# Two-layer graph attention on one core: new step lists, a fold in five steps and an earlier check of the last graph

## The chip, the cores and the metric

The kernel runs on one core of a Trainium2 chip. The core has five engines with queues of their own: TensorE (PE: matmuls, with its weight loads shown apart as PEld), VectorE (DVE), ScalarE (ACT), GpSimd (POOL) and SyncE (SP), which here only issues DMAs. An engine takes its instructions strictly in the order in which the program puts them; engines wait for one another by semaphores. The metric is the device time in microseconds (us) of one launch.

## What is computed

64 graphs of 256 nodes with 512 features pass through two layers. Cut to what matters (LN is a layer norm with gains and offsets):

```
Q, K, V = x @ W_q + b_q, x @ W_k + b_k, x @ W_v + b_v         # 8 heads of 64
scores  = Q K^T / 8 + a_i + c_j + log(adj + 1e-9)
x       = softmax(scores) @ V + x                             # layer 0

h       = LN(x; g1, b1) @ W1                                  # 8 heads of 64
e       = leaky_relu(h.a_src1[i] + h.a_dst1[j], 0.2) + adj
x1      = softmax(e) @ h + x                                  # layer 1, first attention
h2      = LN(x1; g2, b2) @ W2                                 # 1 head of 512
out     = softmax(leaky_relu(h2.a_src2[i] + h2.a_dst2[j], 0.2) + adj) @ h2 + x1
```

All of it is in 32-bit floats.

## The kernel before

**Tiling.** A graph's features lie transposed in `xT` (128 partitions x 4 chunks x 256 nodes). Five products with 512x512 weights (V, Q, K, and V1, V2 of the two norms' attentions) are done by `winograd` (from line 309): seven block products instead of eight, each of 256 columns, on three PSUM banks a, b, c. After product 1 ScalarE copies bank a away (`m1`; line 528 for K, 642 for V1 and V2), and product 6 then adds onto the same bank, so TensorE waits there for the copy. Products 1, 5, 2, 6, 3 make the first step of such a product, product 7 the second and product 4 the third ("K", "K7", "K4").

**Steps.** `graph(b)` (from line 480) is a generator: each `yield` ends a step, and one graph has 42 of them: load, turn (transposes of x and adj), V, V7, V4, Q ..., K4, two times scores (16 matmul records each, then four Exps, line 602, on ScalarE), two times mask (line 616, product with adj on DVE), sums 0, product 0 (line 428), gather 0 (line 437 and 441, then the norm's statistics: lines 257 to 264), tokens 1 (a small matmul, line 267, and eight small DVE operations, then a power on GpSimd, line 291, which give `rstd`), V1 ..., rows 1, eight times weights (Relu line 679, sum with adj line 685 on DVE, Exp line 689), sums 1, product 1, gather 1, tokens 2, V2 ..., rows 2, weights 2 (line 747), and two times product 2 (line 759), whose result is scaled on ScalarE (line 767), added on GpSimd (line 768) and stored by SP (line 771).

**Lists.** `start`, `period` and `finish` (from line 775) say in which order the steps of different graphs are traced. In `period` an entry (age, step) stands for the graph that began that many periods ago; the 42 entries run once per graph. TensorE's instructions stay in exactly this order (`tc.manual_schedule`); those of the other engines are ordered by the compiler's own scheduler, which takes the traced order as their priority. So a place in a list is a place in TensorE's queue, and a rank on the other engines and on SP.

**Fold of the norms.** `fold_norm` (from line 165) multiplies W1 and W2 with the norms' gains once, at the start, in three steps: transpose (row vectors by DMA, four products on GpSimd at line 183, four sums on DVE at line 187), columns (32 matmul records, line 199, and several small DMAs) and totals (eight scalings, line 232, `combine`, line 130, and one transpose).

**Check.** The fast path holds only for inputs in a certain range. `skew`, `rinvs` and `seen` collect values that tell it; `note_odd` folds them into `odd`, and the last lines (907 to 912) make `count` from it, which every engine loads at line 915 to run or skip a slower loop over the graphs. `count` is 0 here.

**Buffers** that matter: adj transposed (`AT`) has four, the Exp tiles (`ET`) four, PSUM a ring of eight banks, Q's and K's tiles are reused by the masks' totals.

Of the kernel before, what the change touches and what calls it, by code (L numbers as in the profile page):

```python
# [9 lines left out]
F32 = mybir.dt.float32  # L10
# [4 lines left out]
P = 128  # L15
# [5 lines left out]
def kernel(  # L21
# [69 lines left out]
    skew = const.tile([P, NT], F32, name="skew")  # L91
    nc.gpsimd.memset(skew, LOW)
# [58 lines left out]
    with ExitStack() as main:  # L151
# [13 lines left out]
        def fold_norm(name, w, g, b, sources, targets, heads):  # L165
# [13 lines left out]
            for kk in range(2):  # L179
                blocks = w[:, kk, :4, :HD].rearrange("p (k n) f -> p k n f", n=2)  # L180
                for i, row in enumerate(vectors):
# [4 lines left out]
                    by_head = product.rearrange("p k n f -> p k (n f)")  # L186
                    nc.vector.tensor_reduce(
# [3 lines left out]
            yield  # L191
# [37 lines left out]
            for kc in range(KC):  # L229
                for n in range(2):  # L230
                    block = w[:, kc % 2, BLOCKS[kc // 2, n], :]
                    nc.vector.scalar_tensor_tensor(
                        block, block, g[:, kc : kc + 1], mean[:, n], ALU.mult, ALU.subtract
                    )
            combine(w)
# [131 lines left out]
        def note_ends(ends):  # L367
            v = ends.rearrange("p t i h -> p (t i h)")
            to = small.tile([P, 4 * H], F32, name="unused", tag="unused", bufs=1)
            note(v, AF.Square, to[:, : v.shape[1]])  # L370

        def note_odd(v, low, high):
# [4 lines left out]
            nc.vector.tensor_tensor(bad, bad, v, ALU.not_equal)  # L377
            nc.vector.tensor_reduce(worst, bad, AX.X, ALU.max)
# [101 lines left out]
        def graph(b):  # L480
# [41 lines left out]
            if b > 0:  # L522
                turn_adj()
            left = left_factors(xT, "xS")
# [218 lines left out]
            note_ends(ends)  # L743
# [8 lines left out]
            for t in range(NT):  # L752
                o = X2[:, t, :]

                for n in (1, 0):
# [9 lines left out]
                    cols = slice(n * HD, (n + 1) * HD)  # L765
                    weighted = work.tile([P, HD + H], F32, name="weighted", tag="kept", bufs=4)[:, :HD]
# [3 lines left out]
                for a in range(4):  # L770
                    nc.sync.dma_start(out=rows[a], in_=o[32 * a : 32 * a + 32, :])
# [4 lines left out]
            (3, "V1 4"), (5, "tokens 2"), (2, "scores"), (2, "scores"), (1, "V4"),  # L776
            (3, "rows 1"), (2, "mask"), (5, "V2"), (3, "weights"), (2, "mask"),
            (5, "V2 7"), (2, "sums 0"), (2, "product 0"), (5, "V2 4"), (1, "Q"),
            (5, "rows 2"), (1, "Q7"), (4, "sums 1"), (2, "gather 0"), (3, "weights"),
            (3, "weights"), (3, "weights"), (5, "weights 2"), (4, "product 1"),  # L780
            (0, "turn"), (1, "Q4"), (1, "K"), (1, "K7"), (3, "weights"),
            (5, "product 2"), (1, "K4"), (5, "product 2"), (3, "weights"),
            (2, "tokens 1"), (0, "V"), (2, "V1"), (3, "weights"), (4, "gather 1"),
            (2, "V1 7"), (0, "V7"), (-1, "load"), (3, "weights"),
# [4 lines left out]
            (0, "Q7"), (0, "Q4"), (1, "load"), (1, "turn"), (0, "K"), (0, "K7"),  # L789
            (0, "K4"), (1, "V"), (1, "V7"), (0, "scores"), (0, "scores"), (2, "load"),  # L790
            (0, "mask"), (0, "mask"), (1, "V4"), (1, "Q"), ("w1", "transpose"),
            (0, "sums 0"), (0, "product 0"), (1, "Q7"), (1, "Q4"), (1, "K"), (1, "K7"),
            ("w1", "columns"), (3, "load"), (1, "K4"), (1, "scores"), (0, "gather 0"),
            (2, "turn"), (0, "tokens 1"), ("w1", "totals"), (2, "V"), (0, "V1"),
            (2, "V7"), (0, "V1 7"), (2, "V4"), (0, "V1 4"), (1, "scores"),
            ("w2", "transpose"), ("w2", "columns"), (0, "rows 1"), (1, "mask"),
            (1, "mask"), (3, "turn"), (1, "sums 0"), (0, "weights"), (1, "product 0"),
            (2, "Q"), (2, "Q7"), (4, "load"), (0, "weights"), (0, "weights"),
            (0, "weights"), (0, "weights"), (2, "Q4"), (2, "K"), (1, "gather 0"),
            (2, "K7"), (2, "K4"), (2, "scores"), ("w2", "totals"), (1, "tokens 1"),  # L800
            (3, "V"), (0, "weights"), (0, "weights"), (2, "scores"), (3, "V7"),
            (0, "weights"), (2, "mask"), (1, "V1"), (1, "V1 7"), (0, "sums 1"),
            (1, "V1 4"), (4, "turn"), (1, "rows 1"), (3, "V4"), (2, "mask"),
            (2, "sums 0"), (0, "product 1"), (3, "Q"), (1, "weights"), (2, "product 0"),
            (1, "weights"), (1, "weights"), (3, "Q7"), (3, "Q4"), (2, "gather 0"),
            (1, "weights"), (3, "K"), (1, "weights"), (3, "K7"), (3, "K4"),
            (1, "weights"), (2, "tokens 1"), (4, "V"), (2, "V1"), (1, "weights"),
            (5, "load"), (2, "V1 7"), (1, "weights"), (4, "V7"), (0, "gather 1"),
        ]
        FOLDS = [(w, step) for w in ("w1", "w2") for step in ("transpose", "columns", "totals")]  # L810
# [7 lines left out]
            (-4, "V1 4"), (-6, "tokens 2"), (-3, "scores"), (-3, "scores"), (-6, "V2"),  # L818
            (-3, "mask"), (-3, "mask"), (-6, "V2 7"), (-4, "rows 1"), (-2, "V4"),
            (-4, "weights"), (-3, "sums 0"), (-3, "product 0"), (-6, "V2 4"),  # L820
# [304 lines left out]
```

## Time and profile before

| | us |
|---|---|
| median of 3 runs | 3231.83 (3231.08 to 3232.96) |
| the profiled execution's own time | 3238.18 |
| its span, first to last instruction | 3236.2 |
| mean granted TensorE clock | 0.991 |
| one graph in the middle, V to V of the next, mean of graphs 6 to 55 | 48.67 |
| ScalarE's Relus, line 679: x1024, mean 0.500 | 460.9 busy |
| DVE's sums with adj, line 685: x512, mean 0.711 | 363.3 busy |
| last product of the last graph ends | 3225.13 |

The profile is one execution, so its times are compared with its own 3238.2 us. A timeline line has the start in us from the span's start, the length, the engine, the line of the kernel, the operation, output and inputs by name, shape and count; in brackets the idle time before it and who ended it. Lines of the chain of waits have a start, a length and who held the chain. A line of waits has who waited, for whom, us in all, times and the longest.

### The profile page before, as it was taken

What the parts mean: (1) busy time and instruction counts of PE and PEld (TensorE: products, weight loads), DVE (VectorE), ACT (ScalarE), POOL (GpSimd) and SP (SyncE); (2) the same over time, 40 slices, a digit from 0 to 9 for tenths busy, and PEclk for the clock granted to TensorE, in tenths of its full rate; (3) what the DMA queues carried; (4) which work ended last, traced back from release to release, by engine and by line L of the source; (5) the groups of instructions that cost most, each with busy time, mean ns of one, the idle gap of its engine ahead of it and who ended that gap; (6) DMA issues with size and microseconds to landing.
All of it is one profiled execution on the core that took longest, in us unless ns stands there. A gap on an engine that the chain in (4) does not pass through costs nothing. (4 is left out here: it accounts for less than half of the span.)

```text
span 3236.2 us, 77633 instructions
## 1 busy us (share of the span) xinstructions
PE 3138.6 (97%) x28240; PEld 2627.2 (81%) x28240; DVE 2662.2 (82%) x6025; ACT 2187.6 (68%) x5959; POOL 899.3 (28%) x1250
## 2 busy tenths in 40 slices
PE   7899999999999999999999999999999999999985
PEld 5678888888888888888888888888888888888864
DVE  5888888888888888888888888888888888888874
ACT  3567667667677667677677677677677677677663
POOL 2232232232232232232232232222222222222332
PEclk9999999999999999999999999999999999999998
DMA  4333443443444444444443443444444444444332
GB/s 132 105 115 122 134 132 122 133 131 123 130 132 125 127 136 125 130 131 126 133 132 122 125 134 127 125 133 128 126 130 130 128 128 132 128 129 131 121 110 79
DMA packets 354341, 407.66 MB, mean 126 GB/s; under 512 B 117776, under 2 KB 262176, under 8 KB 353952
## 3 DMA queue, kind: packets, MB, share of 16 engines
q1 hardware_dynamic: 352800, 401.56, 40.4%
q8 instruction: 225, 3.69, 0.5%
q14 instruction: 164, 1.34, 0.1%
q10 hardware_dynamic: 1152, 1.06, 0.1%
HBM read 266.57 MB, written 135.87 MB: 124 GB/s over the span
## 5 line engine op out<-in xcount | busy, mean ns | idle before, releaser
L685 DVE TENSOR_TENSOR ET<-ET,AT 128x512 f32<-128x512 f32 x512 | 363.3, 711 | 241.3 <-ACT ET L679 240.8
L689 ACT ACTIVATE ET<-ET,ends 128x256 f32<-128x256 f32 x1024 | 482.6, 503 | 105.9 <-DVE ET L685 105.0
L679 ACT ACTIVATE ET<-R,f 128x256 f32<-128x256 f32 x1024 | 460.9, 500 | 69.0 <-PE ps_num L428 57.1
L428 PE MATMUL ps_num<-ET,V 128*32 128x256 f32 x8192 | 466.7, 379 | 0.0
L428 PEld LDWEIGHTS ps_num<-ET,V 128*32 128x32 f32 x8192 | 263.9, 110 | 155.1 <-issue 1.0
L301 POOL TENSOR_TENSOR S<-yT 128x256 f32<-128x256 f32 x64 | 47.8, 747 | 1204.3 <-ACT zT L412 1006.5
L768 POOL TENSOR_TENSOR X<-X,weighted 128x256 f32<-128x256 f32 x256 | 211.1, 836 | 574.8 <-ACT weighted L767 574.7
L616 DVE TENSOR_TENSOR ET<-ET,AT 128x1024 f32<-128x1024 f32 x256 | 307.3, 1232 | 36.3 <-ACT ET L602 36.3
L602 ACT ACTIVATE ET<-ps_sc,V 128x512 f32<-128x512 f32 x512 | 302.8, 698 | 7.5 <-PE ps_sc L595 7.4
L325 PE MATMUL ps_a<-w,S 128*128 128x264 f32 (+1 forms) x1024 | 269.6, 386 | 9.4 <-ACT m L642 5.2
L325 PE MATMUL ps_b<-w,S 128*128 128x264 f32 (+1 forms) x1024 | 267.4, 384 | 0.0
L759 PE MATMUL ps_av<-V,ET 128*128 128x258 f32 (+1 forms) x1024 | 251.1, 390 | 10.8 <-DVE ET L747 10.8
L262 DVE BATCH_NORM_STATS2 parts<-Z 128x6 f32<-128x128 f32 x1024 | 245.5, 277 | 0.0
L595 PE MATMUL ps_sc<-QT,KT 64*128 64x256 f32 x2048 | 239.4, 383 | 0.0
L325 PEld LDWEIGHTS ps_a<-w,S 128*128 128x128 f32 x1024 | 189.0, 190 | 48.7 <-ACT m L642 8.6
L325 PEld LDWEIGHTS ps_b<-w,S 128*128 128x128 f32 x1024 | 194.6, 190 | 31.4
L759 PEld LDWEIGHTS ps_av<-V,ET 128*128 128x128 f32 x1024 | 190.0, 196 | 35.3 <-DVE ET L747 11.3
L595 PEld LDWEIGHTS ps_sc<-QT,KT 64*128 64x128 f32 x2048 | 192.5, 187 | 25.0 <-issue 1.7
L649 ACT ACTIVATE V<-ps_a,rstd 128x257 f32<-128x257 f32 (+1 forms) x128 | 60.1, 470 | 199.9 <-PE ps_a L325 199.9
L437 DVE TENSOR_TENSOR ps_num<-ps_num,R 128x512 f32<-128x512 f32 x256 | 169.6, 687 | 4.3 <-DMA R<-kept 4.1
L767 ACT ACTIVATE weighted<-ps_av,rinvs 128x256 f32<-128x256 f32 x256 | 114.4, 472 | 76.8 <-DVE rinvs L764 60.4
L332 PE MATMUL ps_a<-S,wk 128*128 128x128 f32 x1024 | 148.1, 288 | 14.1 <-ACT m L528 13.6
(176 smaller groups left out, 7193.0 us busy)
## 6 DMA issues: line engine op xcount, KB each, us to landing
R<-kept SPq DMA_DIRECT2D x128, 512.0 KB
X<-in_x_dram SPq DMA_DIRECT2D x256, 128.0 KB
kept<-xT SPq DMA_DIRECT2D x64, 512.0 KB
yT<-kept SPq DMA_DIRECT2D x64, 512.0 KB
R<-kept SPq DMA_DIRECT2D x512, 64.0 KB
kept<-yT SPq DMA_DIRECT2D x64, 512.0 KB
kept<-Z SPq DMA_DIRECT2D x64, 512.0 KB
X<-kept SPq DMA_DIRECT2D x512, 64.0 KB
```

What stands on the lines that cost most here:

```text
L262: nc.vector.bn_stats(parts[:, block].rearrange("p h c -> p (h c)"), Z[:, block, :])
L325: nc.tensor.matmul(to, A[:, kk, :], B[:, kk, :], start=(first and kk == 0), stop=(kk == 1), skip_group_check=not first,)
L428: nc.tensor.matmul(num[32 * a : 32 * a + 32, m * N : (m + 1) * N], V[:, j, a // 2, a % 2 * P + q * DH + 32 * m :][:, :32], pair[a // 2][:, ...
L437: nc.vector.tensor_tensor(both, both, R[:, q, :].unsqueeze(1).to_broadcast([P, 2, N]), ALU.mult)
L595: nc.tensor.matmul(banks[h % 2][:, o : o + N], KT[lo : lo + DH, (q + h) // 2, j * P : (j + 1) * P], QT[lo : lo + DH, (q + h) // 2, :], sta ...
L602: nc.scalar.activation(ET[:, j, i::2, :], banks[i].rearrange("p (h n) -> p h n", n=N), AF.Exp, bias=c[:, j, :],)
L616: nc.vector.tensor_tensor(ET[:, j, :, :], ET[:, j, :, :], AT[:, j, :].unsqueeze(1).to_broadcast([P, 4, N]), ALU.mult,)
L679: nc.scalar.activation(ET[:, j, h, :], R[q][:, h, :], AF.Relu, bias=f[:, j, at : at + 1])
L685: nc.vector.tensor_tensor(two, two, AT[:, j, :].unsqueeze(1).to_broadcast([P, 2, N]), ALU.add)
L689: nc.scalar.activation(ET[:, j, i, :], ET[:, j, i, :], AF.Exp, bias=targets[:, j, 4 * q + i : 4 * q + i + 1],)
L759: nc.tensor.matmul(av[:, :width], ET[:, j, t * P : (t + 1) * P], V2[:, j, n, :width], start=(j == 0), stop=(j == NT - 1),)
L768: nc.gpsimd.tensor_tensor(o[:, cols], o[:, cols], weighted, ALU.add)
```

## The change

It changes the following.

- **Fold.** The first step is cut in two (one half of the chunks each: transpose, products), and so is the last (scale, totals). For W2 (one head) the four sums over 1024 elements on DVE become eight ScalarE instructions over 512 elements with an accumulator.
- **Lists.** `start`, `period` and `finish` are new. In `period` one scores step stands between V and V1, tokens 1 stands ahead of the second product 2, and load, turn, mask, weights, gather, rows and weights 2 have other places; nearly all ages are lower by one (load's is not, and one scores step's is lower by two).
- **Last graph.** Its product 2 is scaled and added by one DVE instruction straight from PSUM, and half of its stores are issued by ScalarE. `skew` becomes part of `latest`, with two more columns for the last graph: the largest element of AT, and the sum of squares of its `ends`. They are compared with `limits` after weights 2 (`note_latest`), the larger checks come once all other graphs are traced, and `count` is made ahead of the last product 2.

```diff
+    latest = const.tile([P, NT + 2], F32, name="latest")
+    nc.gpsimd.memset(latest, LOW)
+    skew = latest[:, :NT]
+    limits = const.tile([P, NT + 2], F32, name="limits")
+    nc.gpsimd.memset(limits, 0.0)
+    nc.gpsimd.memset(limits[:, NT : NT + 1], 400.0)
+    nc.gpsimd.memset(limits[:, NT + 1 :], 30.0)
...
                     by_head = product.rearrange("p k n f -> p k (n f)")
+                    if heads == 1:
+                        for k in range(2):
+                            nc.scalar.activation(
+                                by_head[:, k], by_head[:, k], AF.Identity,
+                                accum_out=w[:, kk, 2 * k + i, HD:],
+                            )
+                        continue
                     nc.vector.tensor_reduce(
...
-            yield
+                yield
...
                         block, block, g[:, kc : kc + 1], mean[:, n], ALU.mult, ALU.subtract
                     )
+                if kc == 1:
+                    yield
...
+        def note_latest():
+
+            bad = work.tile([P, HD + H], F32, name="bad", tag="kept", bufs=4)[:, : NT + 2]
+            worst = small.tile([P, 1], F32, name="worst", tag="worst")
+            nc.vector.tensor_tensor(bad, latest, limits, ALU.min)
+            nc.vector.tensor_tensor(bad, bad, latest, ALU.not_equal)
+            nc.vector.tensor_reduce(worst, bad, AX.X, ALU.max)
+            nc.vector.tensor_tensor(odd, odd, worst, ALU.max)
...
+            if last:
+                nc.vector.tensor_reduce(
+                    latest[:, NT + 1 :], AT.rearrange("p j n -> p (j n)"), AX.X, ALU.max
+                )
...
-            note_ends(ends)
+            note_ends(ends, latest[:, NT : NT + 1] if last else None)
...
+                    if last:
+                        nc.vector.scalar_tensor_tensor(
+                            o[:, cols], av[:, :HD], rinv[:, t : t + 1], o[:, cols],
+                            ALU.mult, ALU.add,
+                        )
+                        continue
...
-                    nc.sync.dma_start(out=rows[a], in_=o[32 * a : 32 * a + 32, :])
+                    queue = nc.scalar if last and a % 2 else nc.sync
+                    queue.dma_start(out=rows[a], in_=o[32 * a : 32 * a + 32, :])
...
         period = [
-            (3, "V1 4"), (5, "tokens 2"), (2, "scores"), (2, "scores"), (1, "V4"),
-            (3, "rows 1"), (2, "mask"), (5, "V2"), (3, "weights"), (2, "mask"),
-            (5, "V2 7"), (2, "sums 0"), (2, "product 0"), (5, "V2 4"), (1, "Q"),
-            (5, "rows 2"), (1, "Q7"), (4, "sums 1"), (2, "gather 0"), (3, "weights"),
-            (3, "weights"), (3, "weights"), (5, "weights 2"), (4, "product 1"),
-            (0, "turn"), (1, "Q4"), (1, "K"), (1, "K7"), (3, "weights"),
-            (5, "product 2"), (1, "K4"), (5, "product 2"), (3, "weights"),
-            (2, "tokens 1"), (0, "V"), (2, "V1"), (3, "weights"), (4, "gather 1"),
-            (2, "V1 7"), (0, "V7"), (-1, "load"), (3, "weights"),
+            (2, "V1 4"), (4, "tokens 2"), (-1, "load"), (1, "scores"), (1, "mask"),
+            (3, "weights"), (0, "V4"), (1, "mask"), (4, "V2"), (4, "V2 7"),
+            (2, "rows 1"), (2, "weights"), (1, "sums 0"), (1, "product 0"), (4, "V2 4"),
+            (0, "Q"), (4, "rows 2"), (0, "Q7"), (2, "weights"), (2, "weights"),
+            (3, "sums 1"), (1, "gather 0"), (3, "product 1"), (2, "weights"), (0, "Q4"),
+            (-1, "turn"), (4, "weights 2"), (0, "K"), (0, "K7"), (4, "product 2"),
+            (0, "K4"), (1, "tokens 1"), (2, "weights"), (2, "weights"),
+            (4, "product 2"), (-1, "V"), (0, "scores"), (2, "weights"), (1, "V1"),
+            (3, "gather 1"), (1, "V1 7"), (-1, "V7"),
         ]
...
         start = [
             (0, "load"), (0, "turn"), (0, "V"), (0, "V7"), (0, "V4"), (0, "Q"),
-            (0, "Q7"), (0, "Q4"), (1, "load"), (1, "turn"), (0, "K"), (0, "K7"),
-            (0, "K4"), (1, "V"), (1, "V7"), (0, "scores"), (0, "scores"), (2, "load"),
-            (0, "mask"), (0, "mask"), (1, "V4"), (1, "Q"), ("w1", "transpose"),
-            (0, "sums 0"), (0, "product 0"), (1, "Q7"), (1, "Q4"), (1, "K"), (1, "K7"),
-            ("w1", "columns"), (3, "load"), (1, "K4"), (1, "scores"), (0, "gather 0"),
-            (2, "turn"), (0, "tokens 1"), ("w1", "totals"), (2, "V"), (0, "V1"),
-            (2, "V7"), (0, "V1 7"), (2, "V4"), (0, "V1 4"), (1, "scores"),
-            ("w2", "transpose"), ("w2", "columns"), (0, "rows 1"), (1, "mask"),
+            (1, "load"), (0, "Q7"), (1, "turn"), (0, "Q4"), (0, "K"), (0, "K7"),
+            (0, "K4"), (1, "V"), (2, "load"), (1, "V7"), (0, "scores"), (1, "V4"),
+            (0, "scores"), ("w1", "transpose"), (0, "mask"), (0, "mask"), (1, "Q"),
+            (0, "sums 0"), ("w1", "products"), (1, "Q7"), (0, "product 0"), (1, "Q4"),
+            (1, "K"), (1, "K7"), ("w1", "columns"), (0, "gather 0"), (2, "turn"),
+            ("w1", "scale"), (1, "K4"), (1, "scores"), (0, "tokens 1"),
+            ("w1", "totals"), (2, "V"), (0, "V1"), (2, "V7"), (0, "V1 7"), (3, "load"),
+            ("w2", "transpose"), (2, "V4"), (0, "V1 4"), ("w2", "products"),
+            (1, "scores"), (3, "turn"), (1, "mask"), (1, "mask"), (4, "load"),
+            ("w2", "columns"), (1, "sums 0"), (0, "rows 1"), (0, "weights"),
...
         finish = [
...
-            (-1, "mask"), (-1, "sums 0"), (-1, "product 0"), (-4, "V2 4"),
-            (-4, "rows 2"), (-3, "sums 1"), (-1, "gather 0"), (-2, "weights"),
-            (-2, "weights"), (-3, "product 1"), (-2, "weights"), (-4, "weights 2"),
-            (-2, "weights"), (-4, "product 2"), (-4, "product 2"), (-1, "tokens 1"),
-            (-1, "V1"), (-1, "V1 7"), (-2, "weights"), (-3, "gather 1"),
-            (-2, "weights"), (-1, "V1 4"), (-2, "weights"), (-1, "rows 1"),
-            (-3, "tokens 2"), (-2, "weights"), (-3, "V2"), (-3, "V2 7"), (-2, "sums 1"),
-            (-3, "V2 4"), (-1, "weights"), (-1, "weights"), (-1, "weights"),
-            (-1, "weights"), (-3, "rows 2"), (-3, "weights 2"), (-2, "product 1"),
+            (-3, "weights"), (-4, "V2 7"), (-1, "sums 0"), (-1, "product 0"),
+            (-3, "weights"), (-4, "V2 4"), (-4, "rows 2"), (-3, "sums 1"),
+            (-3, "product 1"), (-2, "weights"), (-1, "gather 0"), (-1, "tokens 1"),
+            (-4, "weights 2"), (-3, "gather 1"), (-2, "weights"), (-4, "product 2"),
+            (-2, "weights"), (-2, "weights"), (-2, "weights"), (-4, "product 2"),
+            (-1, "V1"), (-1, "V1 7"), (-1, "V1 4"), (-2, "weights"), (-1, "rows 1"),
+            (-1, "weights"), (-1, "weights"), (-2, "weights"), (-3, "tokens 2"),
+            (-3, "V2"), (-1, "weights"), (-3, "V2 7"), (-2, "weights"), (-3, "V2 4"),
+            (-1, "weights"), (-3, "rows 2"), (-2, "sums 1"), (-2, "product 1"),
...
         ]
...
-                if (g, name) == (B - 1, "rows 2"):
-
-                    note_odd(rinvs[:, : NT * (B - 8)], 1e-25, 1e25)
+                steps_left[g] -= 1
+                others = sum(n for of, n in steps_left.items() if of != B - 1)
+                passed = passed or (g, name) == (B - 1, "V2")
+                if passed and not others and not noted:
+                    noted = True
+                    note_odd(rinvs[:, : NT * (B - 1)], 1e-25, 1e25)
                     note_odd(seen[:, : 4 * B], -1.0, 1e25)
-                    note_odd(seen[:, 4 * B :], -1.0, 3600.0)
+                    note_odd(seen[:, 4 * B : 6 * B - 1], -1.0, 3600.0)
+                if (g, name) == (B - 1, "weights 2"):
+                    note_latest()
+                if steps_left[B - 1] == 1 and not counted:
+                    assert noted
+                    counted = True
+                    pt = ps("tr")
+                    nc.tensor.transpose(pt[:1, :P], odd, ident)
+                    nc.vector.tensor_reduce(odd[:1, :], pt[:1, :P], AX.X, ALU.max)
+                    nc.vector.tensor_scalar(count[:1, :], odd[:1, :], float(B), None, ALU.mult)
         for g in graphs.values():
             assert next(g, None) is None
-        note_odd(skew, LOW, 0.0)
-        note_odd(rinvs[:, NT * (B - 8) :], 1e-25, 1e25)
-        count = const.tile([P, 1], mybir.dt.int32, name="count")
-        pt = ps("tr")
-        nc.tensor.transpose(pt[:1, :P], odd, ident)
-        nc.vector.tensor_reduce(odd[:1, :], pt[:1, :P], AX.X, ALU.max)
-        nc.vector.tensor_scalar(count[:1, :], odd[:1, :], float(B), None, ALU.mult)
```

The rest of `start` and `finish` holds the same steps in a like order.

## The prediction

> **What bounds the kernel now.** I read the page's totals first, then the windows by stage, then what TensorE waits for, and last the order of its work.
>
> ```profile
> PE 3138.6 (97%) x28240; PEld 2627.2 (81%) x28240; DVE 2662.2 (82%) x6025; ACT 2187.6 (68%) x5959; POOL 899.3 (28%) x1250
> ```
>
> TensorE is busy for 97% of the span, so at most about 98 us could be won without touching a matmul. The windows say where those microseconds are (span from:to, length, then busy us of PE, PEld, DVE, ACT, POOL; granted clock; DMA):
>
> ```profile
> 50.00:100.00 50.00, 37.62 (x310) 29.80 (x309) 39.36 (x65) 15.68 (x41) 26.11 (x17) 0.94 0.33 102
> 100.00:150.00 50.00, 43.55 (x377) 34.47 (x379) 42.66 (x78) 31.37 (x79) 9.28 (x11) 0.93 0.27 88
> ...
> 2500.00:2900.00 400.00, 398.17 (x3641) 335.41 (x3631) 338.92 (x771) 283.16 (x776) 111.31 (x156) 1.00 0.42 130
> ...
> 3100.00:3150.00 50.00, 39.86 (x326) 29.48 (x324) 38.09 (x95) 32.56 (x84) 16.14 (x16) 0.90 0.36 116
> 3150.00:3200.00 50.00, 33.83 (x289) 23.94 (x288) 27.50 (x70) 24.98 (x71) 12.28 (x15) 0.90 0.31 96
> ```
>
> The long middle is full; the first 150 us and the last 140 us are not. What TensorE waited for (total us, times, longest):
>
> ```profile
> PE ps_st L267 <- DVE parts L264: 19.6, 4, 8.2
> PE ps_a L332 <- ACT m L528: 13.6, 22, 1.9
> PE ps_av L759 <- DVE ET L747: 10.8, 4, 6.1
> ```
>
> Asked by window, the first and third lie in the start and the finish; the second is the whole loss of the middle.
>
> TensorE's instructions follow the hand-written lists, so counting them in order gives the start of every step of every graph. One graph takes 48.67 us (mean, graphs 6 to 55), 48.32 at best. Adding the median distance from each step's first matmul to the next one's, with K at its shortest (4.466 us), gives 48.08. So 0.59 us a graph is lost, 0.56 of it in step K (57 graphs, mean 5.03). The cause in one period:
>
> ```profile
> 313.36 1.70 ACT L679 ACTIVATE ET<-R,f 128x256 f32<-128x256 f32 x4
> 314.97 0.89 ACT L689 ACTIVATE ET<-ET,ends 128x256 f32<-128x256 f32 x2
> 315.76 0.60 ACT L561 ACTIVATE QT<-ps_a,columns 128x128 f32<-128x128 f32 x2
> 316.26 0.36 ACT L528 COPY m<-ps_a 128x256 f32<-128x256 f32 x1
> ```
>
> K's product 6 reuses K's first bank, which ScalarE must have copied (L528). That copy stands behind Relus and Exps of "weights" and behind Q4's L561; the bank was complete at about 314.9, the copy ended at 316.6.
>
> **The period: what it costs.** The list is the old one with ages one lower, and on TensorE only two steps change place. One "scores" leaves the pair and goes between V and V1; "tokens 1" goes ahead of the second product 2. A pair and a single of the old trace (TensorE in time order):
>
> ```profile
> 45.77 3.73 PE L595 MATMUL ps_sc<-QT,KT 64*128 64x256 f32 x32
> 49.42 1.14 PE L325 MATMUL ps_a<-wv,xT 128*128 128x257 f32 x4
> ...
> 3113.33 2.00 PE L595 MATMUL ps_sc<-QT,KT 64*128 64x256 f32 x16
> 3115.26 1.13 PE L325 MATMUL ps_a<-w,zT 128*128 128x257 f32 x4
> ```
>
> A pair holds TensorE 3.65 us, a single 1.93, so two singles cost 0.20 more. The step before scores also ends later (V to scores 4.497 us once, against V to V1 4.404), +0.09, and the first product after it takes 0.971 instead of 0.867, +0.10. Together +0.40. V no longer follows the 48-wide matmul of tokens 1 and should take 4.34 instead of 4.40: -0.07. **Floor 48.41, +0.33 a graph**, over about 58 periods +19 us. Here the Trainium skill speaks against the change: "TensorEngine Tiling (Array Packing)", Key Properties, says that changing the tiling mode drains the array. Scores use 64 rows, their neighbours 128, and the split adds two changes. The page gives no price; by the one drain that another page prices, about 128 cycles at 2.4 GHz ("TensorE: Matmul & The Clock Gate", Part 2), two would be an estimated 0.11 us a graph, 6 us in all. The rows have 0.40; I take the rows, since they hold the same shapes.
>
> **The period: what it may bring.** K's wait is bounded at -0.59 (gone) and, if ScalarE's order gets worse, +0.4 (K took 1 us too long in the worse old graphs). I take -0.42. In the old list the fifth weights step stands right after K7 and its Relus run just ahead of K's copy; the new list has no weights step between Q4 and tokens 1, and two of the other four come before "gather 0", so their DVE halves no longer wait behind eight bn_stats of 0.28 us. Also four of the scores' eight Exps (0.57 us each) leave the stretch after tokens 2, and half of the mask work can start sooner, where DVE is full. Net -0.09 a graph: **-5 us**, between -15 and +42.
>
> Three margins of the new order I checked against the rows. Tokens 2 to V2's product 6 shrinks from 7.5 to 5.7 us; rstd ended 3.2 us after tokens 2 in all 50 graphs, and a 0.54 us copy follows: it fits. K4 to V stays at 1.9 us (product 2 and tokens 1 change places) and two xT transposes of 0.67 need 1.35. The "weights 2" step now follows "turn", whose transposes take 2.2 us on DVE; its L747 ended 4.1 us ahead of product 2 in the old order, so some 1.5 us are left. The "load" moves from the list's end to its third place, behind the eight X2 issues of tokens 2 on SP: 24.6 us of TensorE's work ahead of turn instead of 26.5, for X and A that are 2 us of issues each.
>
> **The start.** TensorE waits there, between 60 and 150 us: 3.8 for the fold of W1 (L199), 6.3 for parts (L264), 4.1 for the ACT copy u (L642), 3.0 for the totals (L621), and 1.5 in small ones; after such waits the matmuls run slow, so that from 47.6 to 143.9 us it falls 29.6 us behind the sum of its steps. The change: (a) the W1 fold moves ahead of graph 0's masks and W2's loads move up with (2, load). SP issued the vectors only at 57.8 behind 11.0 us of W2's sixteen DMAs; POOL's products (4 x 2.36 us) began at 61.7, having been idle for 20.7. Begun some 5 us sooner, the 3.8 us wait goes. Behind those DMAs SP holds graph 1's rows and A, not late yet. (b) Layer two's sums leave DVE: 4 x 1.20 us (L187) at 97.5 to 105.8, in a stretch where DVE has hardly any idle time from 73.5 to 104. They become eight ScalarE instructions of 128x512; nearest row 0.72 (L520) plus 0.19 to read the accumulator, 7.3 us on an engine with 31.4 of 50 busy: hidden, and if not, up to 2 us. (c) Steps of five spread DVE's scaling (8 x 0.48) and combining (4 x 0.7, up to 2.7 beside POOL), ahead of which gather 0 now stands: the 4.0 us wait for tokens 1 shrinks. Bounds: -20 (waits and half of the slow clock) and +4 (the sums land before a ScalarE copy). I take **-9**: the 3.8, half of u's and parts' 8.1, and 1 of slow clock.
>
> **The finish.** TensorE's order hardly changes: counted in work left to the end, every step of the last graph's matmuls stays within 1 us but V4, K7 and tokens 1. Tokens 1 now stands ahead of the two product 2 that waited 6.1 us for L747 anyway (parts ready 3136.9, L747 3136.8), so V1 no longer waits for rstd: it took 6.3 us instead of 4.45, -1.9. V2 4 of graph 61 loses its cover (sums 1), +0.6, and sums 1 of graph 62 comes after rows 2 of 61; its R had about 5 us to spare before L437 took it up at 3172.9. The large checks move into V2, where DVE had 4.2 us idle: -0.3. The waits of 8.2 and 5.1 for parts are one chain on DVE that nothing shortens. Sum **-2**, between -8 and +6.
>
> **The tail.** Columns: start, length.
>
> ```profile
> 3225.83 0.70 DVE odd L379
> 3226.53 0.04 issue
> 3226.57 0.28 PE ps_tr L910
> 3226.86 0.02 issue
> 3226.88 0.29 DVE odd L911
> 3227.17 0.02 issue
> 3227.19 0.14 DVE count L912
> ```
>
> TensorE's last product ends at 3225.13; every engine then loads the count at 3227.37, and from there TensorE's branches (3.34 and 2.4 us) carry the end to 3236.2. With the count made ahead, that load follows the last product: -2.2. The transpose between the products costs +0.3; odd is ready, since four DVE operations of 0.15 us follow weights 2 and a product 2 of 3.2 us lies between. ScalarE's 0.47, POOL's 0.72 and two of four 0.43 us DMA issues after the last product become one DVE operation of 0.5: beside TensorE's branches, nothing; behind the two DMAs that wait on ScalarE's queue stands only its load of the count. Graph 63's maximum over AT is one reduce of about 0.6 us: nothing. **-2**.
>
> **Sum**: -5 -9 -2 -2 = -18. The profiled execution took 3238.2 (span 3236.2); against it 3220, against the median of 3231.8 **3213**.
>
> **Rivals.** (1) K's wait stays, since ScalarE's order is left to the scheduler: -5 becomes +19, 3237.5. For it: Q4's copies still follow the fourth weights step. (2) Slower: the early scores' Exps (0.57 us each) get in front of V's and V1's copies on ScalarE, and TensorE waits for one of them in every graph, 0.6 us: 3213 + 35 = 3248. It turns the sign from 0.32 us a graph on. For it: those copies leave little margin, and eight PSUM banks must hold V, scores and V1; against: ScalarE was mostly idle in that stretch. (3) Start and finish give nothing, because a fold begun sooner meets a DVE that is full anyway: 3213 + 11 = 3224. (4) All of K's wait goes and the start gives 18: 3213 - 10 - 9 = 3194.
>
> **How the numbers follow.** Forecast 0.43, (1) 0.17, (2) 0.20, (3) 0.08, (4) 0.12. What this kernel's runs tell from no change is 0.2%, 6.5 us. Faster: forecast, (4) and part of (3), 0.58; same: most of (1), part of (3), 0.19; slower: (2) and the rest of (1), 0.23. Range 3195 to 3246; the forecast's own 3200 to 3226.
>
> **What would show it.** Right: K without L528 waits, a period of 48.4 to 48.6, single scores of 1.93, L199 without a wait, the count ahead of the last L759. Wrong: a wait that recurs in every graph at V, V1 or product 2, or a period above 49.

## The result, and the profile after

| us | before | after |
|---|---|---|
| median, lowest to highest, runs side by side | 3232.39 (3231.08 to 3236.77), 6 runs | 3247.33 (3243.28 to 3250.74), 6 runs |
| the profiled execution: time, span | 3238.18, 3236.2 | 3243.28, 3241.5 |
| a second profiled execution: time, span | 3230.90, 3228.9 | 3242.43, 3240.7 |

The changed kernel is slower: ratio 1.0042, 95% interval 1.0032 to 1.0053, some 15 us; a second comparison gave 1.0038, 1.0024 to 1.0052. The forecast was 18 us faster. The traces themselves differ by less than the medians: 8.5 us, when the two executions of each kernel are averaged. These are the changed kernel's totals, and what its TensorE waited for (total us, times, longest):

```profile
PE 3161.7 (98%) x28240; PEld 2614.3 (81%) x28240; DVE 2655.7 (82%) x6022; ACT 2201.4 (68%) x5971; POOL 896.5 (28%) x1249
```

```profile
PE ps_st L281 <- DVE parts L278: 25.6, 5, 9.1
PE ps_a L346 <- ACT m L558: 9.1, 19, 1.1
...
PE ps_a L339 <- DVE V L570: 3.6, 2, 3.1
...
PE ps_fold L211 <- ACT left L207: 2.4, 1, 2.4
```

Line 558 is the old line 528: K's wait is still there, 9.1 us in 19 graphs where it was 13.6 in 22. TensorE is busy 23 us longer with the same 28240 matmuls. That is the first sign that the loss is no wait at all. The windows (from:to, length, busy us of PE, PEld, DVE, ACT, POOL, then granted clock and DMA) show it again:

```profile
50.00:100.00 50.00, 39.92 (x322) 31.16 (x319) 36.87 (x65) 18.30 (x47) 26.90 (x17) 0.93 0.36 104
100.00:150.00 50.00, 42.83 (x377) 33.84 (x376) 39.34 (x74) 34.79 (x93) 7.96 (x11) 0.93 0.30 91
...
2500.00:2900.00 400.00, 398.29 (x3620) 331.03 (x3610) 331.08 (x753) 280.38 (x768) 108.10 (x152) 1.00 0.41 127
```

In the 400 us of the middle TensorE is as full as before, at full clock, and issues 21 matmuls fewer (3620, before 3641). The start is a little denser: 322 and 377 matmuls in its two windows, before 310 and 377. TensorE's steps, counted in list order, give the ledger. Each figure is the mean of the two executions of a kernel; the last column is the forecast's term.

| stretch, us | before | after | difference | forecast |
|---|---|---|---|---|
| start to V4 of graph 5 | 242.3 | 239.4 | -2.9 | -9 |
| V4 of graph 5 to V4 of graph 58 | 2578.4 | 2596.3 | +17.9 | about -5 |
| from there to TensorE's last product | 400.6 | 399.0 | -1.6 | -2 |
| TensorE's last product to the span's end | 11.2 | 6.4 | -4.8 | -2 |

The split of the two scores steps fills the second row. TensorE of the changed kernel, in order of time, around the two scores of one graph:

```profile
471.92 1.03 PE L339 MATMUL ps_b<-wv,S 128*128 128x257 f32 x4
472.88 2.00 PE L625 MATMUL ps_sc<-QT,KT 64*128 64x256 f32 x16
474.80 1.16 PE L339 MATMUL ps_a<-w,yT 128*128 128x264 f32 x4
...
482.00 0.32 PE L281 MATMUL ps_st<-parts,same 128*128 128x48 f32 x2
482.25 2.00 PE L625 MATMUL ps_sc<-QT,KT 64*128 64x256 f32 x16
484.18 1.13 PE L339 MATMUL ps_a<-wv,xT 128*128 128x257 f32 x4
```

From first matmul to the next step's first, both scores take 1.92 to 1.93 us (474.80 - 472.88, 484.18 - 482.25); in a pair they take 1.83 each. No bracket with idle time stands in any of these lines: the loss is inside busy time.

### The profile page after: what moved, and what is told of

It reads as the page before. It is cut to its first block, busy times and chain, and to the rows that moved or that the text cites. A ratio compares the mean times of both kernels' runs of the same rounds, so it can differ in the third digit from the quotient of the medians.

```text
span 3241.5 us, 77524 instructions
## 1 busy us (share of the span) xinstructions
PE 3161.7 (98%) x28240; PEld 2614.3 (81%) x28240; DVE 2655.7 (82%) x6022; ACT 2201.4 (68%) x5971; POOL 896.5 (28%) x1249
## 3 DMA queue, kind: packets, MB, share of 16 engines
q10 hardware_dynamic: 1344, 1.33, 0.1%
## 4 chain that ended last, share of the span: by engine, by line
PE 86%; DMA 4%; ACT 4%; DVE 2%; issue 0%; SPq 0%; POOL 0%; DVEq 0%; ACTq 0%
PE ps_a L339 21%; PE ps_a L346 13%; PE ps_num L454 10%; PE ps_b L339 10%; PE ps_sc L625 7%; PE ps_av L789 7%; PE ps_b L346 6%; PE ps_c L339 5%; PE ps_su L413 4%; DMA R<-kept 4%; PE ps_c L346 3%; ACT ET L709 2%; ACT ET L719 1%; PE ps_st L281 1%; ACT QT L591 0%
## 5 line engine op out<-in xcount | busy, mean ns | idle before, releaser
L719 ACT ACTIVATE ET<-ET,ends 128x256 f32<-128x256 f32 x1024 | 475.9, 503 | 101.4 <-DVE ET L715 101.3
L625 PE MATMUL ps_sc<-QT,KT 64*128 64x256 f32 x2048 | 256.9, 390 | 0.0
L438 ACT ACTIVATE yT<-yT,columns 128x256 f32<-128x256 f32 x256 | 120.9, 499 | 77.4 <-DMA yT<-kept 77.4
L315 POOL TENSOR_TENSOR S<-zT 128x256 f32<-128x256 f32 x63 | 48.7, 773 | 447.5 <-PE ps_a L339 442.4
```

Of the source, the lines that this page charges most:

```text
L625: nc.tensor.matmul(banks[h % 2][:, o : o + N], KT[lo : lo + DH, (q + h) // 2, j * P : (j + 1) * P], QT[lo : lo + DH, (q + h) // 2, :], sta ...
L719: nc.scalar.activation(ET[:, j, i, :], ET[:, j, i, :], AF.Exp, bias=targets[:, j, 4 * q + i : 4 * q + i + 1],)
```

## The experiments

The letters in the expectations: A, the split of the scores costs TensorE its time; C, K waits for Q4's copies; E and F, K waits because R lands late.

**The split alone.** The changed kernel with the pair put back, and the kernel before with nothing but the split:

```diff
+        for g in range(4, 60):                      # e1_pair, on the changed kernel
+            order.remove((g, "scores"))
+            order.insert(order.index((g, "scores")), (g, "scores"))
+        for g in range(5, 60):                      # e2_split, on the kernel before
+            order.remove((g, "scores"))
+            order.insert(order.index((g + 1, "V")) + 1, (g, "scores"))
```

> The changed kernel with the two scores steps of graphs 4 to 59 next to each other again; all else of the change stays. Theory A (each split of the pair costs TensorE 0.40 us in tile-mode changes, and that is what made the change slower): the graph-to-graph time falls from 48.98 to about 48.6 us, 56 graphs x 0.40 = -22 us, so about 3225 us, 7 below the kernel before. Rival B (the new ranks of weights, gather and mask on ScalarE and DVE are what costs; the split is hidden): the time stays at 3243 to 3250 us.

> The kernel before with one change: the first scores step of graphs 5 to 59 stands after the next graph's V, as in the new period. Theory A: +0.40 us a graph for 55 graphs, about 3254 us, single scores of 1.93 us. Rival B: no more than 3 us slower, about 3233 us.

With the pair back the changed kernel took 3233.52 us, 0.9990 of before (0.9979 to 1.0000), and its mean period 48.70 us in place of 48.98. The split alone took 3260.23, ratio 1.0074 (1.0059 to 1.0090): 24 us, against 55 graphs times the 0.40 us of the forecast, 22. Its best period rose from 48.32 to 48.74. So the split is the loss, shown from both sides, and the rest of the change is worth about 3 us (0 to 7). The pair brought back 17 us and not the 22 of the forecast: scores, V and V1 fell by 0.20, 0.10 and 0.12 us a graph, but K's mean was 5.07 us, 0.13 above the first trace of the changed kernel. With the new lists and the pair together, then, K waits as long as before the change.

**The code without the new lists**, that is before's three lists with the new fold steps next to their old neighbours, and **Q4 behind K's products** in the kernel before:

```diff
+        for g in range(4, 62):                      # e4_q4
+            order.remove((g, "Q4"))
+            order.insert(order.index((g, "K")) + 1, (g, "Q4"))
```

> The changed kernel's code (fold in five steps with its new steps next to their old neighbours, layer two's sums on ScalarE, last graph's check and stores) with the three lists of before. If the lists alone cost and the code alone gains: the end after the last product shrinks from 11.1 to about 6.6 us and the sums leave DVE, -4 to -8 us, about 3226 us. If the code costs too (ScalarE's sums in front of copies): 3232 us or more.

> The kernel before with step Q4 of graphs 4 to 61 moved from ahead of K to behind K's first five products; TensorE's work is the same. Theory C (K's product 6 waits because Q4's two ScalarE copies, 0.6 us, stand in front of the copy of K's first bank): K's excess falls from 0.56 to 0.2 us or less a graph, -15 to -25 us, about 3212 us. Rival D (the Exps of the fourth weights step alone hold the copy up): K's excess stays above 0.45 us, 3226 to 3236 us.

The code alone: 3236.20 us, ratio 0.9997 (0.9989 to 1.0006); its tail was 8.1 us in place of 11.2 and its start 1 us later (V2 of graph 5 at 438.5, before 437.5). Q4 moved: 3236.92, 0.9999 (0.9988 to 1.0010), K's mean 5.18 us in place of 5.05. Theory C falls: K waits just as long when Q4's copies no longer stand in front.

**What K waits for.** Two graphs of the kernel before, one after the other. ScalarE, then TensorE, in order of time; the brackets hold the idle time before a line and who ended it:

```profile
1722.05 1.69 ACT L679 ACTIVATE ET<-R,f 128x256 f32<-128x256 f32 x4
1723.64 0.89 ACT L689 ACTIVATE ET<-ET,ends 128x256 f32<-128x256 f32 x2
1724.44 0.60 ACT L561 ACTIVATE QT<-ps_a,columns 128x128 f32<-128x128 f32 x2
1724.94 0.36 ACT L528 COPY m<-ps_a 128x256 f32<-128x256 f32 x1
...
1770.14 0.91 ACT L689 ACTIVATE ET<-ET,ends 128x256 f32<-128x256 f32 x2 [0.65 <-DVE ET L685]
1772.38 1.71 ACT L679 ACTIVATE ET<-R,f 128x256 f32<-128x256 f32 x4 [1.33 <-DMA R<-kept]
1773.99 0.89 ACT L689 ACTIVATE ET<-ET,ends 128x256 f32<-128x256 f32 x2
1774.79 0.60 ACT L561 ACTIVATE QT<-ps_a,columns 128x128 f32<-128x128 f32 x2
1775.29 0.36 ACT L528 COPY m<-ps_a 128x256 f32<-128x256 f32 x1
```

```profile
1725.35 1.16 PE L332 MATMUL ps_a<-S,wk 128*128 128x128 f32 x8
...
1775.70 0.49 PE L332 MATMUL ps_a<-S,wk 128*128 128x128 f32 x2 [1.95 <-ACT m L528]
```

The order on ScalarE is the same in both graphs. In the second, ScalarE has stood 0.65 us for VectorE, and then its Relus of heads 4 to 7 stand 1.33 us before an R that has not landed; K's copy stands behind both, and TensorE pays 1.95 us. R alone is the usual case, and it holds in every graph of 6 to 55: each wait of TensorE above 0.15 us has a wait for R on ScalarE right ahead of it (1.07 after 1.03, 0.78 after 0.74, 0.63 after 0.59), and graphs without the one have less than 0.12 of the other. (In the second executions it holds in 17 of 19 such graphs of before and 17 of 17 of the changed kernel; in the other two ScalarE was late after a wait of 0.6 us for VectorE.) In the changed kernel the order and the wait are the same (here graph 48; graph 21: 1.05 after 1.02):

```profile
2367.66 1.71 ACT L709 ACTIVATE ET<-R,f 128x256 f32<-128x256 f32 x4 [0.88 <-DMA R<-kept]
2370.98 1.16 PE L346 MATMUL ps_a<-S,wk 128*128 128x128 f32 x8 [0.92 <-ACT m L558]
```

R is issued on SP (L476) only when sums 1 has freed its buffer, and that hardly varies: in the first trace of before the issue stands about 4.3 us ahead of K, and the Relus come up for it as a rule 3.8 us after the issue. What varies is the landing. The trace has it in sixteen parts: the last landed 3.4 to 5.8 us after the issue, the fifteenth never later than 4.3. In the graph with 1.95 us, fifteen had landed after 3.8 us and the last after 5.8. Why one part is late in some graphs stays open.

**R sooner, by a fourth buffer** (X2 gives up one for the space, which e8 tries alone; two of the fold's vectors move to another buffer):

```diff
-    [P, n, N], F32, name="R", tag="R" if n == 4 else "R1", bufs=3 if n == 4 else 1
+    [P, n, N], F32, name="R", tag="R" if n == 4 else "R1", bufs=4 if n == 4 else 1
-            X2 = data.tile([P, NT, D], F32, name="X2", tag="X2", bufs=2)
+            X2 = data.tile([P, NT, D], F32, name="X2", tag="X2")
```

> The kernel before with a fourth buffer for the row tiles R, so that the second half of rows 1 need not wait for sums 1; the room comes from X2, which has one buffer instead of two. Theory E (TensorE waits in K because ScalarE, in order, waits for the transfer R<-kept, which is issued only when sums 1 frees the third buffer): the waits on the ACT copy of K's bank vanish, K falls from 5.05 to about 4.7 us a graph, -20 us, about 0.994 of the time before. Rival F (the transfer is late whenever it is issued, by contention): K stays at 5.0 us or more and the time within 3 us.

> The changed kernel with the scores pair restored in graphs 4 to 59 and the fourth R buffer. If the split's tile-mode changes and the late R are the two costs of the middle and they add: e1_pair's time less some 20 us, about 0.993 of the time before; a period of 48.4 us. If E is wrong: as e1_pair, 0.999.

> The changed kernel with the fourth R buffer, the split left in. Theory A and E together: K's wait goes, the single scores stay at 1.93 us, the period is 48.7 to 48.8 us, about 23 us slower than e6_pair_r4 and about equal to the kernel before. If the split hid behind K's wait, it would now be nearer to e6_pair_r4 than 15 us.

> Control for e5_r4: the kernel before with X2 in one buffer and three R buffers as before. All theories: no change, within 3 us of the kernel before; K at 5.0 to 5.15 us.

TensorE's waits in e5_r4, and ScalarE's wait for R, from 400 to 2900 us (total, times, longest):

```profile
PE ps_a L332 <- ACT m L561: 44.9, 50, 2.3
PE ps_a L332 <- ACT u L561: 25.8, 48, 0.5
PE ps_a L332 <- ACT m L528: 1.9, 4, 0.8
```

```profile
ACT ET L679 <- DMA R<-kept: 137.1, 50, 4.2
```

K's wait is gone, 1.9 us where it was 12.4, and yet the kernel is slower by a ratio of 1.037 (1.0352 to 1.0387). The wait for R has moved and grown: the scheduler that orders ScalarE now puts Relus ahead of Q's copies, where R has not landed either, so ScalarE stands before it for 137.1 us in place of 9.3, and Q took 6.33 us in place of 4.46 on average. That is the same mechanism in another place. It does not show what K would gain from an R that is there in time, since R's issue and ScalarE's order changed together. On the changed kernel the buffer gave 1.0325 with the pair and 1.0452 without (1.0310 to 1.0341, 1.0435 to 1.0468), a difference of 41 us for the split where the three-buffer kernels show about 17. Most of the excess is in V1, 4.96 us against 4.45 with the pair, where the split costs 0.12 with three buffers; why stays open. The control without the fourth buffer: 1.0007 (0.9997 to 1.0018).

**The Relus later.** Not the data but the order: the Relus of heads 4 to 7 are queued on ScalarE behind the second copy of K.

```diff
...
+                    behind = k_copies.get(b + 2) if q == 1 else None
+                    with tc.issue_after(behind.ins) if behind else nullcontext():
+                        for j in range(NT):
+                            nc.scalar.activation(
+                                ET[:, j, h, :], R[q][:, h, :], AF.Relu, bias=f[:, j, at : at + 1]
+                            )
...
```

> The kernel before with one constraint on ScalarE's order and nothing else: the Relus of a graph's heads 4 to 7 (the ones that need the second R) are queued behind the first two copies of the K product of the graph two later. Theory F (K's wait is ScalarE standing in its queue before a Relu whose R has not landed): K on TensorE falls from a mean of 5.05 us to 4.8 or less, the waits on the copy m L528 in 400 to 2900 us fall from 12.4 us to under 2, the mean period from 48.7 to 48.35-48.45, the time by 58 x 0.3 = 17 us to about 3220 (ratio 0.9945). Rival G (the delayed Relus are themselves needed: the wait only moves, to K's third copy, to the copies of V or to sums 1 of the next period): period within 0.1 of 48.7 or above, a new row of 10 us or more among TensorE's waits, ratio 1.000 or above.

> The changed kernel with both scores products of a graph put side by side again (graphs 4 to 59) and with the Relus of heads 4 to 7 queued behind the first two copies of K. Theory F: the two add up; the kernel with the pair alone stood at 0.999 of before, K's wait was 0.36 us per graph in it, so about 58 x 0.3 = 17 us less: ratio 0.9935 (3216 us), period 48.35-48.45, scores 1.83 each. Rival G: ratio 0.998 to 1.003, period 48.7, K short but a new wait elsewhere.

TensorE's waits in e9_pin, and one of ScalarE's, from 400 to 2900 us:

```profile
PE ps_a L326 <- ACT m L649: 33.7, 49, 0.7
PE ps_a L326 <- DVE V L658: 26.6, 49, 0.9
PE ps_a L333 <- ACT u L533: 14.8, 49, 0.3
...
PE ps_a L333 <- ACT m L533: 3.4, 8, 1.1
```

```profile
ACT yT L413 <- DMA yT<-kept: 162.7, 49, 4.2
```

Rival G, and far beyond it: 1.0396 (1.0382 to 1.0410). K's first copy costs 3.4 us in place of 12.4, but V1 takes 0.95 us more and V7 0.71 in every graph, and Q and K itself 0.22 each on average. With the pair in the changed kernel it was 1.0339 (1.0323 to 1.0355); there V7 alone lost 1.73 us a graph to VectorE (L688). ScalarE's order changed far beyond the Relus: it now stands 162.7 us before the load of yT, 12.1 before. So these runs show what the constraint costs, and not what K's wait is worth; by which chain the delayed Relus reach V1 and V7 was not traced.

**The same data in two halves**, so that the first Relus need only the first:

```diff
-                nc.sync.dma_start(out=R, in_=kept[q : q + n, :].partition_broadcast(P))
+                step = 2 if q == 4 else n
+                for k in range(0, n, step):
+                    nc.sync.dma_start(
+                        out=R[:, k : k + step], in_=kept[q + k : q + k + step, :].partition_broadcast(P))
```

> The kernel before with the load of the second R (heads 4 to 7, 512 KB) issued as two loads of two heads each and nothing else; ScalarE's order stays as it was but for one Relu a place earlier. Theory F (K waits because ScalarE stands before the first Relu of heads 4 to 7 until R has landed): the first half lands about 1 us sooner than the whole, K on TensorE falls from 5.05-5.17 to 4.8-4.9, the waits on m L528 (its line moves by a few) fall from 12.4 us to 3-6, the time by 58 x 0.2 = 12 us (ratio 0.996). Rival J (a load's landing is set by its fixed part, or by the queue of the DMA engines, not by its bytes): the halves land when the whole did, one more issue on SP costs 0.4 us per graph that nobody waits for: ratio 0.999 to 1.002, K unchanged.

> The changed kernel with the pair of scores side by side and R's second load in two halves. Theory F: the pair's 0.999 and 12 us less: ratio 0.995 (3217 us), scores 1.83, K 4.8 to 4.9. Rival J: 0.999, as with the pair alone.

ScalarE's wait for R in the kernel before, then in e13_halves, and TensorE's in e13_halves, from 400 to 2900 us:

```profile
ACT ET L679 <- DMA R<-kept: 9.3, 18, 1.3
```

```profile
ACT ET L684 <- DMA R<-kept: 30.8, 48, 1.3
```

```profile
PE ps_a L332 <- ACT u L533: 15.5, 51, 0.5
PE ps_a L332 <- ACT m L533: 15.3, 39, 1.1
```

Both expectations missed: 1.0106 (1.0091 to 1.0122), and 1.0082 (1.0068 to 1.0095) on the changed kernel with the pair. The first half did land sooner, 3.3 us after its issue (median), the second 4.2. But the first Relu now stands two Exps earlier, so it comes up for its half about 1.2 us sooner, and ScalarE waits for R in nearly every graph. K's mean rose by 0.48 us, and 0.40 of it is something else: one Relu more stands ahead of K's third copy, so that the last of K's five products takes 1.35 us in place of 0.95. So this run, too, changed ScalarE's order along with the data. What carries the account of K's wait is the match from graph to graph, in both kernels; no experiment took the wait away with ScalarE's order left as it was.

**The start: the fold's vectors on another queue**, in the changed kernel, and all of it together:

```diff
-                nc.sync.dma_start(out=row, in_=a.rearrange("h d -> (h d)").partition_broadcast(P))
+                nc.scalar.dma_start(out=row, in_=a.rearrange("h d -> (h d)").partition_broadcast(P))
```

> The changed kernel with the fold's four vector loads on ScalarE's DMA queue in place of SP's, so that they do not stand behind W2's sixteen pieces. Theory H (the start gave 3 us and not 9 because the vectors still came late): POOL's first product begins at 52 us or earlier in place of 62.3, the waits on w1's columns on TensorE fall from 3.7 us to under 1, the first V2 of graph 5 begins 3 us earlier, the time is about 3 us under the changed kernel's (ratio to before 1.003). Rival I (another wait of the start takes its place: V4 of graph 2 behind VectorE, the parts of the statistics): products earlier, but V2 of graph 5 within 1 us of the changed kernel's, ratio 1.004 to 1.005; a loss if the loads delay ScalarE's first copies or if the products take VectorE's time earlier.

> All three: the changed kernel with the pair of scores, the Relus behind K's copies and the vectors on ScalarE's queue. Theory F with H: ratio 0.9925 (3212 us). F with I: 0.9935, as without the vectors. G: 0.998 or above.

First SP and POOL of the changed kernel, then POOL and VectorE of e11_vec:

```profile
47.16 11.15 SPq L128 DMA_DIRECT2D w<-in_L_gnn_W_dram  x16
58.35 0.58 SPq L182 DMA_DIRECT2D vector<-in_L_gnn_a_src_dram  x1
...
59.51 0.54 SPq L422 DMA_DIRECT2D kept<-inverse  x1
```

```profile
62.30 6.97 POOL L188 TENSOR_TENSOR product<-w,vector 128x1024 f32<-128x1024 f32 x3 [21.14 <-issue]
```

```profile
43.45 7.98 POOL L188 TENSOR_TENSOR product<-w,vector 128x1024 f32<-128x1024 f32 x3 [2.23 <-DMA w<-in_L_gnn_W_dram]
```

```profile
46.76 6.89 DVE L646 TENSOR_TENSOR ET<-ET,AT 128x1024 f32<-128x1024 f32 x3 [1.93 <-ACT ET L632]
```

In the changed kernel the vectors are issued at 58.35 us; before it was 57.8. The new place of the fold in the list did not bring its data sooner, and POOL began at 62.30 where it had begun at 61.7. With the vectors ahead of W2, POOL began at 43.45, as theory H had it, and the waits for w1's columns went. Its products now ran beside the first masks on VectorE, which took 2.30 us each and not 1.21, and sums 0 waited 6.5 us for them. These two nearly cancel: TensorE reached the first scores of graph 1 at 78.63 us, 0.7 us later than the changed kernel. There it stopped for 18.6 us, for the parts of graph 0's statistics, and SP shows why. SP of e11_vec, and what it waited for from 40 to 100 us:

```profile
50.64 30.93 SPq L128 DMA_DIRECT2D w<-in_L_gnn_W_dram  x16
81.67 0.54 SPq L422 DMA_DIRECT2D kept<-inverse  x1
```

```profile
SPq L128 <- DMA vector<-in_L_gnn_a_src_dram: 10.4, 1, 10.4
SPq L128 <- DMA vector<-in_L_gnn_a_dst_dram: 9.8, 1, 9.8
```

Layer two's vectors now stand in ScalarE's queue, which issued them at 58.37 and 77.68 us; W2's sixteen loads on SP waited for both to land and took 30.9 us in place of 11.2, and graph 0's sums, behind them on SP, were stored at 81.67 in place of 59.51. V2 of graph 5 began at 451.4 and not 436.2. Rival I's loss, but for a reason that neither theory had: ratio 1.0091 (1.0077 to 1.0105), 15 us more than the changed kernel. All three edits together: 1.0392 (1.0377 to 1.0408).

**Another execution of each kernel:**

> The changed kernel itself, another execution. Theory L (K's wait varies between executions, and the first profile of the changed kernel was a lucky one, the lowest of its six times): K's mean is 5.0 to 5.15 and not 4.94, the mean period 49.05 to 49.15, the rest as in the first trace, the span 3245 to 3252. Theory M (the rest is elsewhere): K's mean is 4.94 again, and the span with it 3241.

> The kernel before itself, another execution. Theory L: K's mean between 4.95 and 5.2, its difference from the 5.05 of the first trace times 58 is the span's difference. Theory M: K 5.05 as before, span 3236 within 2 us.

K's mean was 4.99 us in a2 (first trace 4.94), 5.03 in b2 (5.05), the mean periods 49.01 and 48.64. Neither theory holds as written. What did change is the finish of the kernel before: from V4 of graph 58 to its last product 398.0 us in b2 and 403.2 in the first trace. The first pair of traces would have credited the new finish with 3.5 us; the mean of two leaves 1.6, less than the executions differ. The kernel before against itself gave 0.9991 (0.9982 to 0.9999), so a thousandth is the limit of these comparisons. The traces' 8.5 us are at the lower end of the second interval (8 to 17 us) and below the first (10 to 17); both profiled executions of the changed kernel were at or next to the lowest of their runs, and the first one of before, 3238.18, was above all six of its runs. So the other 3 to 6 us lie in which executions were profiled; in which stage a slower one loses them, no trace shows.

## Why the prediction was wrong

**The step that failed: "I take -0.42" for K's wait.** It fell by 0.08 us (5.04 to 4.96, means of two executions; two executions of one kernel differ by up to 0.05), and the net of the period, forecast at -0.09 a graph, became +0.33. Two things were wrong. First the cause: I read the Relus and Exps ahead of K's copy as work whose rank the list sets, and reasoned from the new ranks of the weights steps. The list sets TensorE's order only. ScalarE's is the scheduler's, and around K it came out the same in both kernels: four Relus, two Exps, Q4's two copies, K's copy. What varies is whether the Relus find R: its issue hangs on sums 1, which did not move against K, and its landing varies by 2.4 us. The bracket "DMA R<-kept" stands in the trace of before; my own example, at 313 us, was a graph without it. Second the size: I set K's loss at 0.56 us against 4.466, the shortest K. That is the K of graphs 0 to 3 and 63. In the steady graphs the last three of its five products take at least 0.98, 0.99 and 0.95 us, where those take 0.89, even when no wait is listed, so the shortest steady K is 4.71 and the wait only 0.34. The best period of 48.32, which I quoted beside it, said so: it lies 0.24 above my floor of 48.08.

**The floor** was right in kind and small by 0.07: +0.33 forecast, about +0.40 measured. The scores' 0.20 came as read off, and so did the 0.10 of the product behind them (V1 +0.11) and V's balance (+0.03 against +0.02). Missing was the second product 2, which now follows the 48-wide matmul of tokens 1 in V's place: 1.736 to 1.805, +0.07. What leaves one step behind such a matmul puts another there. The Trainium skill's drain at a change of tiling mode ("TensorEngine Tiling (Array Packing)", Key Properties) bears on the row: the page names no price, the prediction's estimate was 0.11 us a graph, and e2_split measured 24 us / 55 = 0.44. Taking the trace's rows there was right; how much of the 0.44 is that drain, no run here separates.

**The start** gave -2.9 and not -9. The 4.1 us wait for u did go, but the forecast had the fold some 5 us sooner by its place in the list, while SP's order kept its vectors behind W2's sixteen pieces; a wait of V4 behind VectorE (3.1) came in, and the waits for W1's fold, which were to go, grew from 3.8 to 6.1. Rival 3 had the size of this, but not the reason: the fold did not begin sooner. Whether one that does would gain is open, since e11_vec, which began it 19 us sooner, held up SP's loads.

**The finish** gave -1.6 against -2, but two executions of the kernel before differ by 5.2 there, so this term is neither confirmed nor refuted. **The tail** gave -4.8 against -2: beside the earlier load of the count, one of the two long stretches at TensorE's branches, 2.4 us, shrank to 0.1. The count was indeed ahead of the last products:

```profile
3229.39 2.86 PE ps_av L789 x8
3232.25 0.21 PE ps_tr L947
3232.47 2.46 PE ps_av L789 x8
3234.93 0.02 issue
3234.96 0.48 DVE X L797
```

The chain of waits of the changed kernel now ends with the output itself, not with the check; the transpose between the products costs 0.2. In e1_pair and e3_code, with the same tail code, the tail was 8.6 and 8.1 us, so some 2 us of the gain depend on the rest of the program and not on this edit.

Of the rivals, the first (K's wait stays, since ScalarE's order is left to the scheduler) named the mechanism; its 3237.5, with the 6 us that the start did not give, comes to some 3244. The second, copies of V behind the early Exps, did not come: V and V1 grew by no more than the terms of the floor, and no wait at V1 is listed from 260 to 2900 us. "A period above 49" was the sign named for wrong; the two traces have 48.98 and 49.01.

No kernel here beats the one before by more than its comparisons can tell; the nearest is the change with its pair restored, 0.999. Whether the start, the finish and the tail could be kept without their effect on ScalarE was not tried further.

## What to carry to other kernels

Before a wait is credited to a new list, ask whose order the list sets: find what the *waiting* engine's queue stood for in the graphs where the wait was long, and compare with one where it was short. Moving a step next to another kind of matmul has a price even where TensorE shows no idle time: look up what the same shapes cost singly and in pairs, multiply by the graphs, and pay that first. Bringing data or an engine's work forward can cost more than the wait it removes, when a scheduler then places the consumer ahead of what the busiest engine needs. And before a load is moved to another queue, ask when that engine gets round to issuing it, and what on the old queue waits for it.

## What was not expected of the hardware

The last part of one and the same 512 KB load of R landed between 3.4 and 5.8 us after its issue; where it passed the 3.8 us or so at which the Relus came up for it, K waited. A VectorE operation of 128x1024 took 1.21 us alone and 2.3 us while POOL multiplied tiles of that size. And a wait too short to be listed has a second price: in graph 35 of before (K at 1722.58 us), 0.08 us of waiting stood ahead of K's product 6, and that product's first matmul then took 0.21 us in place of 0.11.
